# Writing attention planes and normalised-input planes to DRAM from ScalarE's queue instead of SyncE's

## The chip, the cores and the metric

The kernel runs on one core of one Trainium2 chip. The metric is the device time of one execution in microseconds; the time given for a kernel is the median of its runs.

A core has a matrix engine (TensorE, PE in the profile; its weight loads are PEld), three engines for element-wise work (VectorE or DVE, ScalarE or ACT, GpSimd or POOL), and SyncE (SP), which only issues transfers. Every engine works through its own instructions in the order in which the program gives them. Transfers between on-chip memory (SBUF) and DRAM are issued by one of the engines and then carried out by 16 DMA engines.

## The reference

Two layers, each with a pre-normalisation and a residual, on x of 128 batches x 128 nodes x 512 features in float32. The first mixes the nodes with a normalised adjacency matrix, the second is graph attention with 8 heads and an additive mask.

```python
h = relu(layernorm(x))
x = x + norm_adj @ (h @ W0) + b0
h = relu(layernorm(x))
q, k, v = (h @ Wq + bq), (h @ Wk + bk), (h @ Wv + bv)     # 8 heads of 64
attn = softmax(q k^T / 8 + (1 - adj) * -1e9)
x = x + (attn @ v) @ Wo + bo
```

## The kernel before, in words

The 128 batches go in 32 groups of four (`GB`). A group takes part in four dense products with 512 x 512 weights: first the layer-0 weight (block W), then q, k and v (blocks Q, K, V) and the output projection (block Y). Each product is a two-level fast matrix multiplication with seven block products, so a block has seven steps, Q0 to Q6 and so on; each step has a place before it (Q3) and places after its products (Q3b). All five products share the lines L388 (PE), L429 and L439 (VectorE adds block results out of the PSUM banks a, b, c, d) and, for q, k and v, L711, L714 and L725 (ScalarE takes the first result out of a bank).

Time runs in slots t. In slot t the blocks are W for group t + 1, Q, K and V for group t, and Y for group t - 1. Beside these dense blocks lie the smaller steps of neighbouring groups, put by hand into places (`at(t, place, f, ...)`). The scheduler is switched off (`manual_schedule`), so the order of each engine's instructions is the order in which these calls are made.

The names and lines on which the text below relies:

- `load_x` (L161, SP) loads half a group of x, two batches, two groups ahead into one of eight buffers. `store_half` (L838, SP) stores half a group of the result; the load of a later group takes the buffer that such a store frees.
- `ln1` (L314 and after, VectorE; L320 and L322, GpSimd) makes the statistics of the first normalisation, and `gcn_norm` (L333, ScalarE) the normalised batch `h`. `gcn_mix` (L605, PE) multiplies `h`, loaded as weights, with the adjacency matrix into `pa`; L610 (ScalarE) copies it out. In slots 2 to 29 `gcn_norm` for the four batches of group t + 2 stands at Q3, Q4, Q5b and Q6, `gcn_mix` at Q5, Q6, K1 and K2.
- `scores` (L754 PE; L758 or L761) and `row_max` (L773) begin the softmax; `exponentials` (L781, ScalarE, eight heads one by one with their sums) and `softmax_end` (L788 VectorE, L789 GpSimd) finish it.
- The normalised attention weights have to be transposed[...]. So `split_att` has ScalarE copy the float32 weights of a batch into two planes of 16-bit halves, which overwrite the attention buffer of the batch before (L794), and then sends the planes to DRAM (L795). `turn_att` (L798, SP) brings them back transposed. `attend` (L820, PE) uses them in block V of the next slot.
- In steady slots the planes of batch 0 and 1 of group t are split in block Y of that slot (Y3b) and in block W of the next (W1b), and those of batches 2 and 3 in the next slot at Q3b and Q5b. Some batches at the beginning and at the end are transposed on PE instead (`turned_in_place`).
- `split_h` and `turn_h` do the same for batches 0 and 1 of the input of attention: copies at L682 into one common pair of planes (places V2b and V3), after the second of which the planes go to DRAM (L684); L689 brings them back transposed.
- `reload_w` (L1004, SP) loads weights again in four parts each, into two buffers in turn, as PE lets their parts go.
- `Operands.combine` (L362 to L365, L90, GpSimd in steady slots) adds and subtracts operand blocks for the fast multiplication; `add_bias` (L337) and `add_mask` (L769) also run on GpSimd.

All transfers of the kernel before are issued from SP, in one order. A transfer's issue waits on SP until its source is ready and its destination is free, and whatever stands behind it on SP waits as well.

Of the kernel before, what the change touches and what calls it, by code (L numbers as in the profile page):

```python
# [93 lines left out]
def kernel(  # L94
# [16 lines left out]
    nc = tc.nc  # L111
# [36 lines left out]
    planes_dram = [dp.tile([P, 2, H * P], U16, tag=f"planes_{b}", name=f"planes_{b}") for b in range(GB)]  # L148
    h_dram = dp.tile([P, 2, H * P], U16, tag="planes_h", name="planes_h")
# [527 lines left out]
    def split_h(g, b):  # L677


        h2 = hs.pop((g, b)).bitcast(U16).rearrange("n (c f z) -> n z c f", c=NC, z=2)  # L680
        planes = att_of(g - 1, -1).bitcast(U16).rearrange("n h k -> n (h k)")
        nc.scalar.copy(planes.rearrange("n (z c j f) -> n z c j f", z=2, c=NC, j=2)[:, :, :, b, :], h2)  # L682
        if b == 1:
            nc.sync.dma_start(h_dram, planes.rearrange("n (z f) -> n z f", z=2))  # L684

    def turn_h(g):
        op_h[g] = op_norm
# [47 lines left out]
    def att_of(g, b):  # L735


        return att_buf[(b - g) % (GB + 1)]
# [52 lines left out]
    def split_att(g, b):  # L791
        halves = att_of(g, b).bitcast(U16).rearrange("q h (k z) -> q z (h k)", z=2)
        planes = att_of(g, b - 1).bitcast(U16).rearrange("q h k -> q (h k)").rearrange("q (z j) -> q z j", z=2)
        nc.scalar.copy(planes, halves)  # L794
        nc.sync.dma_start(planes_dram[b], planes)  # L795

    def turn_att(g, b):
        nc.sync.dma_start_transpose(out=att_of(g, b - 1).bitcast(U16), in_=planes_dram[b].rearrange("q z j -> (q z) j"))  # L798
# [49 lines left out]
    for t in range(-1, NG + 1):  # L848
# [3 lines left out]
        if 0 <= t - 1 < NG - 1:  # L852
            g = t - 1

            for first, final, place, f, *args in (
                ("W1", "-Y6", "Q0", turn_att, 0),
                ("W4b", "-Y6b", "W1b", split_att, 1),
                ("W5", "-Y3", "W2", exponentials, 2, 0, H // 2),
                ("W6", "-Y4", "W3", exponentials, 2, H // 2, H),
                ("Q0b", "-Y5b", "W4b", softmax_end, 2),  # L860
                ("Q1", "-Y5", "W5", exponentials, 3, 0, H // 2),
                ("Q2", "-Y6", "W6", exponentials, 3, H // 2, H),
                ("Q0", "Q1", "Q2", turn_att, 1),
                ("Q2b", "Q0b", "Q0b", softmax_end, 3),
                ("Q4b", "Q0b", "Q3b", split_att, 2),
                ("Q6b", "Q2", "Q5b", split_att, 3),
                ("K1", "Q2", "K0", turn_att, 2),
                ("K3", "Q5", "K2", turn_att, 3),
            ):
                place = first if t == 1 else final if last else place  # L870
                if f in (split_att, turn_att) and turned_in_place(g, args[0]):
                    continue
                at(t - place.startswith("-"), place.strip("-"), f, g, *args)
            if t == 1:
                at(1, "K3", transpose_att, g, 2)
                at(1, "K5", transpose_att, g, 3)
            elif last:
                at(t, "K1", transpose_att, g, 3)
            for b in (2, 3, 0, 1):
                at(t, "V0", attend, g, b)  # L880
# [15 lines left out]
        elif 1 <= t + 1 < NG and t >= 0:  # L896
            g = t + 1
            at(t, "K0b" if g < NG - 1 else "Q0b", ln2, g, 0)
            at(t, "K3b" if g < NG - 1 else "Q3b", ln2, g, 1)
            if g == NG - 1:  # L900

                places = ("Q3", "Q4", "Q5", "Q5", "Q6", "Q6", "K1", "K2", "K2")
                steps = ((norm_h, 0), (norm_h, 1), (transpose_h, 0), (norm_h, 2), (transpose_h, 1), (norm_h, 3))
                steps += ((transpose_h, 2), (transpose_h, 3))
            else:
                places = ("V1", "V2", "V2b", "V3", "V5", "V6", "Y1", "Y2", "Y5")
                steps = ((norm_h, 0), (norm_h, 1), (split_h, 0), (split_h, 1), (norm_h, 2), (norm_h, 3))
                steps += ((transpose_h, 2), (transpose_h, 3))
                at(t, "Y0", turn_h, g)
            for place, (f, b) in zip(places, steps):  # L910
                at(t, place, f, g, b)
            at(t, places[8], attention_operands, g)
            at(t + 1, "Q3", attention_residual, g, 0)
            at(t + 1, "Q4", attention_residual, g, 1)
# [263 lines left out]
```

## Time and profile before

| | |
|---|---|
| time, median of 3 runs | 2293.26 us (2292.56 to 2294.22) |
| span of the profiled execution | 2291.6 us |
| time of the profiled execution around the span | not recorded |
| granted TensorE clock | 0.998 |
| busy: PE, PEld | 99%, 93% |
| busy: VectorE, ScalarE, GpSimd | 82%, 60%, 81% |
| SP's DMA queue (q1) | 448336 packets, 560.08 MB, 80.6% of 16 engines |
| plane writes issued on SP | L795: 121 of 512 KB, 4.5 us to landing; L684: 29 of 512 KB, 3.0 us |

The profile is of one execution. Its times run from the start of its first instruction. "Busy" is the share of the span in which an engine worked on an instruction; issuing a transfer doesn't count as busy. A timeline line gives the start, the length, the engine, the source line, the operation, what it writes and reads, and in brackets how long its engine stood idle before it and what ended that. A line of the list of waits gives who waited for whom: microseconds in total, times, the longest.

### The profile page before, as it was taken

The numbers are of one execution on the slowest core, as the hardware profiler recorded it, in microseconds if no ns is written. First come the engines' busy times: TensorE is split into PE (matmuls) and PEld (weight loads), VectorE is DVE, ScalarE is ACT, GpSimd is POOL, SyncE is SP. The second block draws the span as 40 slices with busy tenths as digits, with TensorE's granted clock in tenths as the row PEclk, the third lists the DMA queues.
The fourth block names the chain that finished last, engine by engine and source line by source line (L and its number), as shares of the span: only waits on it lengthen the run. The fifth ranks groups of instructions, "written<-read, shape, count | busy, mean of one in ns | idle before, by whom it ended". The sixth has DMA issues, their size and how long they took to land.

```text
span 2291.6 us, 50617 instructions
## 1 busy us (share of the span) xinstructions
PE 2273.9 (99%) x18151; PEld 2132.9 (93%) x18151; DVE 1868.3 (82%) x4832; ACT 1364.3 (60%) x3556; POOL 1860.9 (81%) x1927
## 2 busy tenths in 40 slices
PE   9899999999999999999999999999999999999999
PEld 8899999999999999999999999999999999999998
DVE  7877888888888788887888888888888888888876
ACT  3555565655656556656556565565665665655654
POOL 6899788878888788888888887879888888878854
PEclk9999999999999999999999999999999999999999
DMA  5388978889887889878898788998888987889872
GB/s 169 157 259 245 298 231 256 239 251 280 250 252 241 254 254 276 257 247 236 251 297 243 250 238 250 270 258 260 244 246 252 291 253 236 243 245 291 239 242 81
DMA packets 448587, 563.32 MB, mean 246 GB/s; under 512 B 326352, under 2 KB 333648, under 8 KB 447824
## 3 DMA queue, kind: packets, MB, share of 16 engines
q1 hardware_dynamic: 448336, 560.08, 80.6%
q8 instruction: 144, 2.36, 0.4%
q14 instruction: 107, 0.88, 0.1%
HBM read 358.68 MB, written 122.68 MB: 210 GB/s over the span
## 4 chain that ended last, share of the span: by engine, by line
PE 88%; POOL 3%; DMA 3%; DVE 3%; issue 1%; ACT 1%; SPq 0%; POOLq 0%; DVEq 0%; ACTq 0%
PE bank_a L388 31%; PE bank_d L388 19%; PE bank_c L388 10%; PE bank_b L388 10%; PE pa L605 5%; PE bank_d L754 3%; PE po L820 3%; DMA xt<-in_x_dram 2%; PE pss L754 1%; PE bank_b L820 1%; PE bank_a L820 1%; PE bank_b L754 1%; PE pt L674 1%; POOL xt L337 1%; DVE xt L429 1%
## 5 line engine op out<-in xcount | busy, mean ns | idle before, releaser
L781 ACT ACTIVATE att<-att,nmx 128x128 f32<-128x128 f32 x1024 | 396.3, 391 | 0.9 <-DVE nmx L773 0.9
L388 PE MATMUL bank_a<-op_h,w 128*128 128x256 f32 x1488 | 352.0, 379 | 0.0
L789 POOL TENSOR_TENSOR att<-att,rsm 128x1024 f32<-128x1024 f32 x128 | 242.7, 1897 | 82.3 <-DVE rsm L788 82.3
L388 PEld LDWEIGHTS bank_a<-op_h,w 128*128 128x128 f32 x1488 | 268.9, 190 | 29.0
L429 DVE TENSOR_TENSOR xt<-xt,bank_d 128x512 f32<-128x512 f32 x732 | 269.0, 416 | 19.0 <-DVE xt L429 0.9
L794 ACT COPY att<-att 128x2048 uint16<-128x2048 uint16 x121 | 229.3, 1895 | 66.0 <-POOL att L789 66.0
L333 ACT ACTIVATE h<-xt,nb,rs 128x512 f32<-128x512 f32 x254 | 207.2, 817 | 57.8 <-POOL nb L322 56.1
L711 ACT ACTIVATE q<-bank_a,bqk 128x256 f32<-128x256 f32 x192 | 80.4, 470 | 263.0 <-PE bank_a L388 263.0
L320 POOL TENSOR_TENSOR rs<-ve,mhalf 128x2 f32<-128x2 f32 (+1 forms) x129 | 91.4, 708 | 176.2 <-DVE ve L319 175.8
L388 PE MATMUL bank_d<-op_h,w 128*128 128x128 f32 (+1 forms) x1712 | 218.2, 279 | 0.7 <-issue 0.3
L90 POOL TENSOR_TENSOR op_o<-op_o 128x256 f32<-128x256 f32 x297 | 209.6, 729 | 10.0
L388 PEld LDWEIGHTS bank_d<-op_h,w 128*128 128x128 f32 x1712 | 204.0, 193 | 5.1 <-issue 3.1
L90 POOL TENSOR_TENSOR op_a<-op_a 128x256 f32<-128x256 f32 x279 | 196.8, 729 | 14.1 <-DVE op_a L365 4.5
L90 POOL TENSOR_TENSOR op_h<-op_h 128x256 f32<-128x256 f32 x270 | 190.4, 729 | 12.2 <-DVE op_h L365 2.9
L781 ACT ACTIVATION_READ_ACCUMULATOR att<-att,nmx 128x1 f32 x1024 | 194.1, 190 | 0.0
L314 DVE BATCH_NORM_STATS2 st<-xt 128x6 f32<-128x512 f32 x256 | 173.0, 676 | 18.4 <-DMA xt<-in_x_dram 18.3
L388 PE MATMUL bank_a<-w,op_o 128*128 128x256 f32 x768 | 181.7, 379 | 0.0
L388 PE MATMUL bank_a<-w,op_h 128*128 128x256 f32 x744 | 179.1, 384 | 0.0
L388 PE MATMUL bank_a<-w,op_a 128*128 128x256 f32 x744 | 176.1, 380 | 0.0
L439 DVE TENSOR_TENSOR xt<-bank_a,xt 128x512 f32<-128x512 f32 x252 | 167.2, 684 | 10.2 <-PE bank_a L388 2.7
L761 DVE SCALAR_TENSOR_TENSOR att<-bank_d,msk 128x512 f32<-128x512 f32 x128 | 82.5, 686 | 104.4 <-PE bank_d L754 96.8
L773 DVE TENSOR_REDUCE nmx<-att 128x8 f32<-128x1024 f32 x128 | 155.0, 1211 | 0.0
(188 smaller groups left out, 5944.3 us busy)
## 6 DMA issues: line engine op xcount, KB each, us to landing
w<-wd_v SPq DMA_DIRECT2D x93, 704.0 KB, 5.5
w<-wd_o SPq DMA_DIRECT2D x93, 704.0 KB, 6.8
w<-wd_q SPq DMA_DIRECT2D x90, 704.0 KB, 6.1
planes<-att SPq DMA_DIRECT2D x121, 512.0 KB, 4.5
w<-wd SPq DMA_DIRECT2D x87, 704.0 KB, 5.4
xt<-in_x_dram SPq DMA_DIRECT2D x63, 512.0 KB, 6.1
out_dram<-xt SPq DMA_DIRECT2D x62, 512.0 KB, 4.2
planes_h<-att SPq DMA_DIRECT2D x29, 512.0 KB, 3.0
```

The source lines that it names most:

```text
L90: engine.tensor_tensor(twice(out), twice(x), twice(y), ALU.subtract if minus else ALU.add)
L314: nc.vector.bn_stats(self.st[:, j, :], self.src[:, j, :])
L333: nc.scalar.activation(h, src[:, j, :], AF.Relu, bias=nb[:, j : j + 1], scale=rs[:, j : j + 1])
L388: nc.tensor.matmul(out, lhsT, rhs, start=start, stop=True, skip_group_check=True)
L429: nc.vector.tensor_tensor(dst, dst, src, f)
L439: nc.vector.tensor_tensor(t, src.rearrange("p (r f) -> p r f", r=2), t, ALU.add)
L605: nc.tensor.matmul(pa[:, c * P : (c + 1) * P], h[:, c * P : (c + 1) * P], ant, start=True, stop=True)
L754: nc.tensor.matmul(pss[p][:, c, :], qs[g][rows, c, cols], ks[g][rows, c, cols], start=True, stop=True)
L773: nc.vector.tensor_reduce(nmx, att_of(g, b), AX.X, ALU.max, negate=True)
L781: nc.scalar.activation(att[:, h, :], att[:, h, :], AF.Exp, bias=nmx[:, h : h + 1], scale=1.0, accum_out=sm[:, h : h + 1])
L789: nc.gpsimd.tensor_tensor(att, att, rsm.unsqueeze(2).to_broadcast([P, H, P]), ALU.mult)
L794: nc.scalar.copy(planes, halves)
```

## The change

Two plane writes change their issuing engine: that of the normalised input (`split_h`) and that of the attention weights (`split_att`). Each call is at the same place in the program, right after the ScalarE copy that makes the planes. The transposing reads (`turn_h`, `turn_att`) stay on SP, as do all other transfers.

```diff
@@ -681,7 +681,7 @@
         planes = att_of(g - 1, -1).bitcast(U16).rearrange("n h k -> n (h k)")
         nc.scalar.copy(planes.rearrange("n (z c j f) -> n z c j f", z=2, c=NC, j=2)[:, :, :, b, :], h2)
         if b == 1:
-            nc.sync.dma_start(h_dram, planes.rearrange("n (z f) -> n z f", z=2))
+            nc.scalar.dma_start(h_dram, planes.rearrange("n (z f) -> n z f", z=2))
@@ -792,7 +792,7 @@
         halves = att_of(g, b).bitcast(U16).rearrange("q h (k z) -> q z (h k)", z=2)
         planes = att_of(g, b - 1).bitcast(U16).rearrange("q h k -> q (h k)").rearrange("q (z j) -> q z j", z=2)
         nc.scalar.copy(planes, halves)
-        nc.sync.dma_start(planes_dram[b], planes)
+        nc.scalar.dma_start(planes_dram[b], planes)
```

In the program as built, ScalarE's order has 150 more instructions, each right behind the copy of L794 or the second copy of L682, and SP's order has 150 fewer. The orders of PE, VectorE and GpSimd are the same as before.

## The prediction

> **What bounds the kernel now.** First the page's busy times, then the lists of waits of TensorE and VectorE.
>
> ```profile
> PE 2273.9 (99%) x18151; PEld 2132.9 (93%) x18151; DVE 1868.3 (82%) x4832; ACT 1364.3 (60%) x3556; POOL 1860.9 (81%) x1927
> ...
> PEld bank_c L388 <- DVE xt L429: 10.9, 16, 4.2
> ...
> PE bank_c L388 <- DVE xt L429: 7.4, 8, 3.8
> ...
> DVE st L314 <- DMA xt<-in_x_dram: 18.3, 19, 2.4
> ```
>
> TensorE (PE) is idle for 2291.6 - 2273.9 = 17.7 us in all, the prologue included. So whatever the change does well can bring back less than 1%, while whatever makes PE wait is lost in full. Its one wait that recurs is for VectorE to empty bank c (L429), and that follows VectorE's wait for x's load: L314 stands in VectorE's order ahead of the read that PE needs.
>
> Next the chain of waits in order of time, by which I measure the period: the same instruction, `po` L820, once per group of four batches.
>
> ```profile
> 846.87 1.90 PE po L820 x32
> ...
> 916.95 1.90 PE po L820 x32
> ...
> 987.02 1.90 PE po L820 x32
> ...
> 1058.28 1.78 PE po L820 x29
> ```
>
> The distances are 70.08, 70.07 and 71.26 us. From 213.09 to 2112.35 us there are 27 such distances: 1899.26 us, against 27 x 70.07 = 1891.89 at the shortest. All that steady stages lose now is 7.4 us, in the groups in which x's load lands late. This is the most that a better DMA order can return there.
>
> Last the place where a delay of ScalarE (ACT) has no cover: the timelines of ACT, of PE's weight loads and of PE around the split of batch 3.
>
> ```profile
> 900.90 0.84 ACT L711 ACTIVATE q<-bank_a,bqk 128x256 f32<-128x256 f32 x2 [0.95 <-PE bank_a L388]
> 901.62 1.90 ACT L794 COPY att<-att 128x2048 uint16<-128x2048 uint16 x1
> 903.41 0.82 ACT L333 ACTIVATE h<-xt,nb,rs 128x512 f32<-128x512 f32 x1
> ...
> 904.29 1.01 PEld L605 LDWEIGHTS pa<-ant,h 128*128 128x128 f32 x8
> ...
> 902.71 1.89 PE L388 MATMUL bank_a<-op_h,w 128*128 128x256 f32 x8
> 904.43 1.05 PE L605 MATMUL pa<-ant,h 128*128 128x128 f32 x8
> ```
>
> Columns are start, length, engine, line. The third `h` of the group ends at 903.41 + 0.82 = 904.23, and the load of it as PE's weights begins at 904.29, 0.06 later: that load waits for `h`. The first product follows 0.14 later, exactly when the product before it lets PE go. At two other places a load stands 0.11 ahead of its first product (907.23 and 907.34), so `h` has 0.14 - 0.11 = 0.03 us to spare. Other groups show the same picture (974.31 and 974.36; 1045.56 and 1045.61; 1115.66 and 1115.71).
>
> **What the Trainium skill says.** "DMA: Bandwidth & Descriptors", section "Issuing engines are not separate DMA queues": whichever engine issues, transfers share the same 16 DMA engines, and another issuer saves only issue time. The trace of before has SP's queue alone, so it can't confirm this. "Perfetto Trace Analysis", section "DMA Instruction — HWDGE (DVE, Sync)": the recorded issue covers a wait for the descriptor generator, locked "for exclusive use", and the generating; moving the data comes after. The trace agrees on the second half: issues of 0.34 us land after 3.0 us. "PSUM — Partial Sum Buffer", section "Engine vs sequencer instructions": ScalarE's queue is strict FIFO. The timeline agrees, in program order throughout. "ScalarE: Activation LUTs", section "What ACT_TABLE_LOAD costs": back-to-back ACTIVATEs overlap by about 93 ns; the trace has 903.52 - 903.41 = 0.11 us.
>
> **The change, part by part.** 150 DMA issues (121 of L795, 29 of L684) leave SP and stand in ACT's order right behind the copy whose result they send. They wait for that copy. Their other waits (an earlier use of the same DRAM plane, and in the third site x's second load, landed by about 898) are over by then. Transfers and bytes stay.
>
> *Price of one issue on ACT.* Before has none there, so I price it from SP's rows.
>
> ```profile
> L795 SPq DMA_DIRECT2D planes<-att x121: 332/428/1507, 113.7 to 2216.1; - x121
> ...
> L798 SPq DMA_TRANSPOSE att<-planes x121: 1555/4079/8754, 118.2 to 2224.3; - x121
> ```
>
> (Minimum/median/maximum in ns.) Lost overlap 0.11; the copy's end to the issue's start 0.05 (903.52 to 903.58 on SP); the issue 0.43, the median; restart 0.05, the gap between two issues on SP (874.31 to 874.36). Sum 0.64 us. From below: with an issue and restart of nothing it is 0.16, never less, because the wait for the copy is certain. From above: 0.11 + 0.05 + 1.51 + 0.15 = 1.8 us, or more if the issue waits for a transpose (rival 2).
>
> *Where it lies.* Normalised input (L684, 860.6 us in the group from 846.87): behind it is the copy of v that PE needs at 862.37; it ends at 861.10, so 1.27 us are spare: covered. The exponentials after it end at 864.2 + 0.6, before VectorE's reciprocal at 864.98: covered. Planes of batches 0 and 1 (copies end at 873.94 and 877.91): ACT idles 7.2 us ahead of the q bias at 891.28 and swallows 2 x 0.64: covered. Batch 2 (copy ends at 898.76): behind it the second `h`, needed at 900.48 and done at 899.47; then ACT idles 0.95 ahead of the L711 at 900.90. 0.64 is covered, above 0.95 it is not. Batch 3 (copy ends at 903.52): no cover, as shown. PE waits 0.64 - 0.03 = 0.61 us, and all that follows moves with it; the fourth `h` is needed at 907.34 and was done at 905.42.
>
> This last site exists where batch 3 is split and the next group is mixed, slots t = 2 to 29: 28 times. 28 x 0.61 = +17 us.
>
> *What SP gains.* From its list of waits:
>
> ```profile
> SPq L684 <- ACT att L682: 471.0, 29, 18.3
> ...
> SPq L795 <- ACT att L794: 144.4, 61, 3.5
> SPq L161 <- DMA out_dram<-xt: 138.8, 28, 6.4
> ```
>
> The first two go from SP. Behind L684 stood the first weight reload (issued at 861.11, its old readers done at 857.7), behind L795 another: they move up by about 3 us into a stretch in which DMA had room (share 0.69 from 872 to 880). The planes of batch 1 go out at 878.5 instead of 880.24. But x's load (L161, issued at 883.34) follows the store of x, which waits for VectorE's last L429, and that does not move. What is late next is that store and the bytes issued from 878 on, the same as before. What disappears is a backlog: planes of batch 0 and a reload, 1.2 MB from 873.97 on, last at the page's 246 GB/s until 879.0, some 0.6 us into that store; moved up, they are through by then. So I expect the load to land about 0.6 us earlier. VectorE's typical wait is 18.3/19 = 1 us, so about half of the 7.4 us goes: -4 us; bounds 0 and -7.4. The transposes of batches 2 and 3 (L798) start no later; their result is needed at 916.88, covered.
>
> *Sum.* +17 - 4 = +13 us on the profiled execution. Its span is 2291.6 us; its own whole time is not recorded, so I take the 1.7 us up to the median of 2293.3 as what lies around the span. 2293.3 + 13 = 2306.
>
> **Rivals.** (1) *Faster, or no change.* SP's queue was the brake and ACT has room: 60% busy, long idle stretches. Then all 7.4 us come back, and the first steady group's 2 us (72.1 against 70.07) too, so -9.4. The deciding point is ACT's delay at batch 3: at its floor of 0.16 it costs 28 x 0.13 = 3.6, net -6, 2287 us. With all the gain, break-even is at 9.4/28 + 0.03 = 0.37 us of delay; the net reaches the 0.2% bound (4.6 us) on the fast side only below 0.2 us. For it: the waits of 471 and 144 us on SP. Against it: most of the 471 hid nothing late on PE, and no plane's issue took under 0.33 us on SP.
>
> (2) *Slower by far: ACT's issue waits for the descriptor generator while SP issues a transpose.* At batch 2 SP is inside one:
>
> ```profile
> 896.97 4.58 SPq L798 DMA_TRANSPOSE att<-planes  x1
> 901.65 0.53 SPq L795 DMA_DIRECT2D planes<-att  x1
> ```
>
> Held from 898.81 to 901.55, ACT would be 2.74 us later: 0.64 + 2.74 - 0.95 = 2.4 beyond the cover, x 28 = +68; 2306 + 68 = 2374 us. If only part of the instruction holds it, some 0.5 us at each of the two sites: (0.19 + 0.5) x 28 = +19, 2325. Against it: the direct issue right behind that transpose took 0.53 us, only 0.19 more than the shortest, so little is queued up at its end.
>
> (3) *Nothing measurable.* An issue on ACT takes about half of SP's (delay 0.35): 28 x 0.32 = 9, less 7.4: +1.6, 2295 us. That the change does nothing is excluded: the order of both queues differs.
>
> **How the numbers follow.** The forecast (slower by 5 to 20 us) has 0.60, rival 2 in either size 0.12, the no-change case 0.16, the faster one 0.12. About 0.2%, 4.6 us, is what a measurement of this kernel can tell from no change. Faster 0.12, same 0.16, slower 0.72. Range: below, into the no-change case with all of the DMA gain, 2291; above, issue rows of 0.53 with a slow restart and no gain (28 x 0.8 = +22) and the smaller size of rival 2, 2326. What is left out is the faster case and the full lock.
>
> **What would show it.** In the changed profile: ACT's own queue with 150 issues near 0.4 us; the third `h` about 0.6 us after the copy's end instead of before it; a new wait of PE or PEld at `pa` L605 on ACT `h` L333, some 28 times and about 17 us in total; a shortest period of 70.7 us; VectorE's wait for x's load halved; ACT's busy time unchanged. I am wrong if `pa` shows no wait (then the issue is cheap or the order has slack that I missed), if ACT's issues are long (rival 2), or if a shorter period appears, which would mean that the present 70.07 us hides a wait for SP.

## The result and the profile after

The changed kernel takes 2299.69 us (median of 7 runs, 2297.68 to 2301.03) against 2292.56 us of the kernel before beside it (7 runs, 2291.01 to 2294.22): ratio 1.0034, 95% interval 1.0023 to 1.0044. It is 7.1 us slower. The profiled execution of it took 2300.85 us with a span of 2299.1 us, so 1.75 us lie around the span, as had been assumed.

The busy times and the two queues, from the page of the changed kernel:

```profile
PE 2276.8 (99%) x18151; PEld 2130.3 (93%) x18151; DVE 1867.7 (81%) x4832; ACT 1372.3 (60%) x3556; POOL 1860.7 (81%) x1927
...
q1 hardware_dynamic: 426736, 481.43, 70.5%
q10 hardware_dynamic: 21600, 78.65, 8.9%
```

A second queue, q10, carries the 78.65 MB of planes. The shares of busy time are the same to a point and don't tell what happened.

The chain of waits of the changed kernel, again the same instruction once per group:

```profile
848.92 1.90 PE po L820 x32
...
919.57 1.90 PE po L820 x32
...
990.11 1.90 PE po L820 x32
...
1060.66 1.90 PE po L820 x32
```

From 213.96 to 2118.93 us there are 27 distances, 1904.97 us, 70.55 on average; 26 of the 27 lie within 0.05 us of that. Before, the shortest was 70.07 and the mean 70.34. So two things happened at once. Every group became 0.48 us longer than the shortest one before, 13.1 us over the 27; and the uneven extra of some groups, 7.4 us before, is gone. The net is 5.7 us; the remaining 1.8 us of the difference of the spans lie in equal parts ahead of the first and behind the last of these groups.

The waits of PE's weight loads and of VectorE say what the two things are. From the changed kernel's lists of waits:

```profile
PEld pa L605 <- ACT h L333: 19.2, 30, 1.2
PEld bank_c L388 <- DVE xt L429: 6.0, 6, 4.2
```

```profile
DVE st L314 <- DMA xt<-in_x_dram: 4.0, 4, 2.5
```

The first line is new: 30 waits for `h`, none of which is in the list of before. VectorE's wait for x's load fell from 19 times to 4, and PE's loads wait for bank c 6 times instead of 16.

Where the new wait arises: the timelines of ScalarE and of PE's weight loads in the group from 848.92.

```profile
903.77 1.90 ACT L794 COPY att<-att 128x2048 uint16<-128x2048 uint16 x1
905.70 0.34 ACTq L795 DMA_DIRECT2D planes<-att  x1
906.08 0.81 ACT L333 ACTIVATE h<-xt,nb,rs 128x512 f32<-128x512 f32 x1 [0.42 <-ACT att L794]
```

```profile
906.95 0.97 PEld L605 LDWEIGHTS pa<-ant,h 128*128 128x128 f32 x8 [0.61 <-ACT h L333]
```

The copy ends at 905.67. The issue starts 0.03 later, takes 0.34, and `h` starts 0.04 after it. Before, `h` started 0.11 ahead of the copy's end. Together `h` is 0.03 + 0.34 + 0.04 + 0.11 = 0.52 us later, of which 0.03 was spare: 0.49 us for PE, against the 0.48 by which the distance grew.

### The profile page after: what moved, and what is told of

Read it like the earlier page. It is cut to its first block, busy times and chain, and to the rows that moved or that the text cites. A ratio compares the mean times of both kernels' runs of the same rounds, so it can differ in the third digit from the quotient of the medians.

```text
span 2299.1 us, 50449 instructions
## 1 busy us (share of the span) xinstructions
PE 2276.8 (99%) x18151; PEld 2130.3 (93%) x18151; DVE 1867.7 (81%) x4832; ACT 1372.3 (60%) x3556; POOL 1860.7 (81%) x1927
## 3 DMA queue, kind: packets, MB, share of 16 engines
q10 hardware_dynamic: 21600, 78.65, 8.9%
## 4 chain that ended last, share of the span: by engine, by line
PE 91%; ACT 5%; DVE 2%; issue 1%; ACTq 0%; DMA 0%; SPq 0%; POOL 0%; DVEq 0%; POOLq 0%
PE bank_a L388 33%; PE bank_d L388 22%; PE bank_b L388 10%; PE bank_c L388 10%; PE pa L605 4%; PE bank_d L754 3%; PE po L820 3%; ACT att L794 2%; PE pt L674 1%; PE pss L754 1%; PE bank_b L820 1%; PE bank_a L820 1%; PE bank_b L754 1%; ACT h L333 1%; ACT q L711 1%
## 5 line engine op out<-in xcount | busy, mean ns | idle before, releaser
L794 ACT COPY att<-att 128x2048 uint16<-128x2048 uint16 x121 | 229.3, 1895 | 65.2 <-POOL att L789 65.2
```

## The experiments

All times are medians; the kernel before ran beside each batch on the same chip (2291.51, 2292.06 and 2291.3 us in the three batches). "Over the shortest" is what 27 distances exceed 27 x 70.07 us by, in the profiled execution: 7.4 us before, 13.1 us after the change.

**Batch 3 back on SP.**

```diff
-        nc.scalar.dma_start(planes_dram[b], planes)
+        (nc.sync if b == 3 else nc.scalar).dma_start(planes_dram[b], planes)
```

> The changed kernel, but the planes of batch 3 are written from SP again; all others stay on ScalarE. Theory (the loss is the one issue ahead of the third h, the gain is x's load landing earlier): PE's wait at pa for h goes, the shortest and the usual period are 70.07 us, x's load keeps its earlier landing, so about 7 us less than before: 2285.5 us (2284 to 2288). Rival A (the loss is spread over all 121 + 29 issues on ScalarE, or comes from two queues sharing the DMA engines): one fifth of the 121 goes, so still above before, 2297 to 2299. Rival B (SP's order is what brings x's load forward, and putting one write back on it undoes that): 2292, period again varying between 70.07 and 71.3.

Measured: 2286.64 us, ratio to the kernel before 0.9978 (0.9969 to 0.9986), 0.3 us over the shortest. The list of waits of its weight loads has 2 waits for `h` instead of 30:

```profile
PEld pa L605 <- ACT h L333: 1.0, 2, 0.9
```

One of the five issues of a group carries the whole loss, and the other four the whole gain. Rival A and rival B both fall.

**Batch 3 alone on ScalarE.** The same condition turned around, in the kernel before.

> The kernel before, but the planes of batch 3 alone are written from ScalarE. Theory: the wait at pa comes in full, 28 x 0.48 = 13 us, and nothing is gained on x's load, so 2292.6 + 13 = 2306 us (2303 to 2308): slower than the changed kernel, though it moves only 29 of 150 writes. Rival A (loss spread over all issues): a fifth of the loss, 2294 to 2296. Rival B (two queues at once are the gain, whatever is on them): about 2299, like the changed kernel.

Measured: 2306.1 us, ratio 1.0063 (1.005 to 1.0075), 14.6 us slower. Its shortest distance is 70.55 and it is 17.7 us over the shortest: the loss, with the late loads of x still there. It moves a fifth of the writes and is slower than moving all.

```profile
PEld pa L605 <- ACT h L333: 18.8, 29, 1.7
PEld bank_c L388 <- DVE xt L429: 9.2, 13, 4.1
```

**All on ScalarE, `h` ahead of the split.** In the changed kernel the steady place of the split of batch 3:

```diff
-                ("Q6b", "Q2", "Q5b", split_att, 3),
+                ("Q6b", "Q2", "Q6", split_att, 3),
```

> The changed kernel with all 150 writes on ScalarE, but in steady slots the split of batch 3 stands one place later, so that ScalarE makes the third h first and then the copy and its write. Theory: the third h is ready at about 902.4 instead of 904.8 in the reckoning of the group from 846.87, PE's wait at pa goes, period 70.07, 2285.5 us (2284 to 2288), the same as with batch 3 on SP. Rival A (the number of issues on ScalarE or the second queue costs time): 2299, as changed. Rival C (the next thing on ScalarE is just as tight: the fourth h or the copy of pa): a new wait of PE at the fourth pa or at bank d, 2289 to 2296.

Measured: 2286.26 us, ratio 0.9977 (0.9968 to 0.9987), 0.5 us over the shortest. Its timeline of ScalarE:

```profile
896.89 0.81 ACT L333 ACTIVATE h<-xt,nb,rs 128x512 f32<-128x512 f32 x1
897.60 1.89 ACT L794 COPY att<-att 128x2048 uint16<-128x2048 uint16 x1
899.51 0.34 ACTq L795 DMA_DIRECT2D planes<-att  x1
899.90 0.58 ACT L610 COPY op_a<-pa 128x512 f32<-128x512 f32 x1 [0.41 <-PE bank_a L388]
900.38 0.81 ACT L333 ACTIVATE h<-xt,nb,rs 128x512 f32<-128x512 f32 x1
```

The third `h` now comes ahead of the copy, the fourth behind the issue, and in the steady groups nothing new waits. So neither the number of issues on ScalarE nor the second queue costs time: only which instruction stands behind the issue.

**Two issues instead of one at batch 3.** In the changed kernel:

```diff
+        if b == 3:
+            for z in range(2):
+                nc.scalar.dma_start(planes_dram[b][:, z, :], planes[:, z, :])
+        else:
+            nc.scalar.dma_start(planes_dram[b], planes)
```

> The changed kernel, but the planes of batch 3 go out in two writes of half the size, both from ScalarE, one behind the other. Theory (PE pays each issue in full): one more issue of 0.34 us and a gap of 0.05, so PE's wait grows by 0.39 x 28 = 11 us to 2310.6 us (2308 to 2313), period about 70.94. Rival D (what PE pays is the draining of the copy, the issue itself overlaps with what follows): unchanged, 2299 to 2301.

Measured: 2317.08 us, ratio to the kernel before 1.0108 (1.0092 to 1.0123), 17.4 us above the changed kernel where 11 were expected. The wait grows, so PE pays the issue itself and rival D falls. The usual distance is 71.04 us, 0.49 more than after the change: the two issues and their gap take 0.82 us where one takes 0.34, and that is 0.09 more than reckoned, because the second one takes at least 0.44.

```profile
911.49 0.82 ACTq L797 DMA_DIRECT2D planes<-att  x2
912.36 0.81 ACT L333 ACTIVATE h<-xt,nb,rs 128x512 f32<-128x512 f32 x1 [0.90 <-ACT att L794]
```

The rest is in a few groups in which the pair took up to 1.92 us, the longest single issue 1.53 us. In some of these SP was inside a transpose and in others not; why they are long is open.

**Only the normalised input on ScalarE.** L684 alone, in the kernel before.

> The kernel before, with the normalised-input planes alone (29 writes) written from ScalarE. Theory: ScalarE has cover at that site and SP's long wait for it hid nothing that is late, so no change: 2291.5 us (2290 to 2293), x's load still late in about half of the groups. Rival E (SP's 471 us of waiting for those planes was the brake): the whole gain, 2286.

Measured: 2291.77 us against 2292.06, ratio 0.9999 (0.999 to 1.0007); VectorE waits for x's load 18 times. SP's longest wait of all, 471 us in total, was worth nothing, and the issue on ScalarE there costs nothing: the cover named for this site held.

**Only batches 0 and 1 on ScalarE.**

```diff
-        nc.sync.dma_start(planes_dram[b], planes)
+        (nc.scalar if b < 2 else nc.sync).dma_start(planes_dram[b], planes)
```

> The kernel before, with the planes of batches 0 and 1 alone (60 writes) written from ScalarE. Theory: these are the writes that stand ahead of x's load on SP, and ScalarE idles 7 us behind them; the whole gain at no cost: 2286.5 us (2285 to 2288), period 70.07. Rival E (the brake was elsewhere on SP): 2290 to 2292.

Measured: 2285.04 us, ratio 0.9969 (0.9958 to 0.9981), 0.6 us over the shortest: the whole gain, and the lowest ratio of the study, though its interval overlaps those of the first and the third run.

**Four issues at batch 2.** Batch 3 on SP, and for batch 2 four writes of a quarter each in place of one:

```diff
+            for k in range(4):
+                z, cols = k // 2, slice(k % 2 * 512, k % 2 * 512 + 512)
+                nc.scalar.dma_start(planes_dram[b][:, z, cols], planes[:, z, cols])
```

> Batch 3 on SP as in the first experiment, all others on ScalarE, and the planes of batch 2 in four writes of a quarter each, one behind the other on ScalarE. Theory (0.95 us of ScalarE's time behind batch 2 are covered, then PE pays in full): one issue delays by 0.53 us and each further one by 0.48, the value of the two-issue run, so 0.53 + 3 x 0.48 = 1.97, of which 1.0 is beyond the cover: 28 x 1.0 = 28 us on top of 2286.6, 2314 us (2308 to 2320), with PE waiting at the second pa of the group. Rival F (every issue on ScalarE in this stretch costs PE): three issues more than in the first experiment, 40 us, 2327. Rival G (cover is larger than that, the wait is only at batch 3): 2286.6.

Measured: 2324.97 us, ratio 1.015 (1.0136 to 1.0164), 38.3 us above the first experiment where the theory had 28 and rival F 40. The median alone would favour the rival; the profile doesn't. The median of its distances is 71.08 us, 1.01 above 70.07, just what the cover of 0.95 leaves (rival F would be 71.5), and PE waits at the second `pa` of the group, as expected:

```profile
983.09 1.16 PE L605 MATMUL pa<-ant,h 128*128 128x128 f32 x8 [0.69 <-ACT h L333]
```

Over 27 distances it has 29.8 us over the shortest, against 0.3 in the first experiment. The other 9 us are outside the steady groups: the first of them begins at 215.94 instead of 211.7 us, behind one wait of PE's loads for `h` of 3.3 us, and 5 us come behind the last, whose cause is open. The reckoning had left both out.

**Only batch 1 on ScalarE.** The condition `b == 1`.

> The kernel before, with the planes of batch 1 alone (31 writes) written from ScalarE, so that the weight reload still waits on SP behind the planes of batch 0. Theory of the prediction (the gain comes from planes of batch 0 and the reload behind it moving up into a stretch in which the DMA engines have room): less than half of the gain, 2289 to 2291.5. Rival H (the gain comes from the write of batch 1 itself, which no longer goes out right ahead of the store and x's load in the same queue): the whole gain, 2286.5.

Measured: 2287.06 us, ratio 0.9978 (0.997 to 0.9986), 1.2 us over the shortest; VectorE waits for x's load 8 times instead of 19:

```profile
DVE st L314 <- DMA xt<-in_x_dram: 5.5, 8, 1.9
```

One write of the five brings 5.0 of the 7.0 us that the sixth run gains over the same runs of the kernel before. That is rival H in the main: the step of the prediction that put the gain on batch 0 and the reload behind it fails. What can be theirs is the rest, 2.0 us.

**Batch 1 earlier, but on SP.** The kernel before, with the place of the split of batch 1 moved so that only SP's order changes:

```diff
-                ("W4b", "-Y6b", "W1b", split_att, 1),
+                ("W4b", "-Y6b", "W0", split_att, 1),
```

> The kernel before, all writes on SP, but in steady slots the write of batch 1 is issued ahead of two weight reloads instead of behind them, so at about 878.8 instead of 880.24 in the reckoning of the group from 846.87; nothing else moves. Theory H1 (on ScalarE the write of batch 1 gains because it goes out earlier): most of the gain of batch 1 alone, about 2287 to 2288.5 us. Theory H2 (it gains because it is out of the queue in which the store and x's load follow): no gain, 2291 to 2293, since the same bytes stand ahead of x's load in SP's queue.

**Batch 1 behind the exponentials, on ScalarE.** The kernel before, with the call that writes batch 1 moved to ScalarE and placed behind the exponentials of batch 2 (cut to the lines that matter):

```diff
-        nc.sync.dma_start(planes_dram[b], planes)
+        if not (b == 1 and 1 < g + 1 < NG - 1):
+            nc.sync.dma_start(planes_dram[b], planes)
...
+        nc.scalar.dma_start(planes_dram[1], planes)
...
+                at(t, "W3", send_planes, g)
```

> The kernel before, with the write of batch 1 alone issued from ScalarE in slots 2 to 30, but behind the eight exponentials that follow its copy, so at about 881 instead of 878.4, later than SP issued it before (880.24). Theory H1 (earlier is what counts): no gain, 2291 to 2294 us. Theory H2 (another queue is what counts): most of the gain, 2286 to 2288.5, with x's load landing about 7.2 us after its issue instead of 8.0.

Measured: the earlier write on SP 2290.23 us, ratio 0.9994 (0.9986 to 1.0002), not to be told from no change, 3.8 us over the shortest in its profile. The write behind the exponentials on ScalarE 2288.08 us, ratio 0.9986 (0.9978 to 0.9995), 2.2 us over the shortest.

The tenth run is not the test that it was meant to be: its write did not go out later than before. Its call stands behind the eight exponentials in the program, but in the trace the issue starts during the third of them, in the group whose first `po` product starts at 843.55:

```profile
872.76 1.90 ACT L794 COPY att<-att 128x2048 uint16<-128x2048 uint16 x1 [2.06 <-POOL att L789]
...
875.35 0.39 ACT L781 ACTIVATE att<-att,nmx 128x128 f32<-128x128 f32 x1
875.52 0.37 ACTq L800 DMA_DIRECT2D planes<-att  x1
875.64 0.19 ACT L781 ACTIVATION_READ_ACCUMULATOR att<-att,nmx 128x1 f32 x1
```

That is 31.97 us after the first `po` product. SP issued this write at 33.4 in the kernel before, here in the group from 846.87:

```profile
880.24 0.44 SPq L795 DMA_DIRECT2D planes<-att  x1
```

So H1 is not refuted by this run. The table has the moment of the write beside the landing of x's first load of a group, means over the 27 steady groups of each trace:

| kernel | batch 1's write issued, us after the first `po` product | x's load, issue to landing, us | over the shortest, us |
|---|---|---|---|
| before | 33.44 on SP | 8.02 | 7.4 |
| batch 1 earlier, on SP | 32.06 on SP | 7.83 | 3.8 |
| batch 1 behind the exponentials | 31.97 on ScalarE | 7.61 | 2.2 |
| batch 1 alone on ScalarE | 31.15 on ScalarE | 7.18 | 1.2 |
| batches 0 and 1 on ScalarE | 31.14 on ScalarE | 7.04 | 0.6 |
| changed kernel | 31.14 on ScalarE | 7.02 | covered by the new wait |

Being earlier on the same queue brings at most a part (ninth run). At nearly the same moment the kernel is 2.15 us faster with the write on ScalarE than on SP (2288.08 against 2290.23 us, side by side on one chip). Whether that is the other queue itself is open: with one issue fewer ahead of them, two weight reloads leave SP 0.5 and 0.9 us earlier than in the ninth run. From ScalarE 0.8 us earlier still, the eighth run gains more. How the queue and the moment share the gain is not shown.

The tenth run shows one more thing. There the issue costs ScalarE nothing: the eighth exponential ends 34.20 us after `po`, as in the kernel before, and at 34.81 in the eighth run, where the issue stands directly behind the copy and has to wait for it.

The load is issued at the same point of the group in all of them (36.5 us after `po`; in the tenth run one group, left out, has it 2.3 us later). The store of x ahead of it lands sooner too: 5.90 us after its issue in the changed kernel, 7.13 before. Not everything does: the group's first store takes 4.36 us instead of 3.47, and x's second load 4.74 instead of 4.14.

## Why the prediction was right, and where its sizes and one reason were not

**Right: the direction, the place and the mechanism.** PE waits at the third `pa` of the group for `h`, behind the issue at batch 3, about 0.5 us in each group. The second experiment shows that issue to cause it, the first and third that nothing else does.

**The price of one issue** was put at 0.64 us from SP's median row of 0.428. It is 0.52: the issue takes ScalarE 0.338 us, in the 121 issues of L795 never over 0.375. SP's median mixed two kinds of rows. The 43 plane writes that stood directly behind another issue of SP took 0.41 us or more, and the other 107 have a median of 0.34; on ScalarE all 150 follow a pause. Of the 0.12 us too much 0.09 is the issue, and 0.03 the two gaps around it (0.03 and 0.04 us instead of 0.05 each). So 28 x 0.49 = 13.7 us instead of 17.

**What SP gains** was put at half of 7.4 us; it is all of it, and x's load lands 1.0 us earlier where 0.6 was reckoned. And its reason failed. The prediction saw the write of batch 1 go out earlier, but took the bytes issued from 878 on to be "the same as before", so that the only gain was a backlog of batch 0 and a reload that moves up. The eighth run leaves both where they were and has 5.0 of the 7.0 us. What helps is that the write of batch 1 leaves its place right ahead of the store and x's load: it goes out on another queue, and 2.3 us earlier, since on SP it stood behind a store and two reloads. There was room for it: from 31 to 36 us after `po` the DMA engines' busy share is 0.87 in the kernel before and 0.96 in the eighth run (means over the 27 steady groups). What counted was when and on which queue the bytes went, not their sum. How the DMA engines share their time between two queues no run shows directly.

Both errors go the same way: +13.7 - 7.4 = +6.3 on the steady groups against +13 predicted, and with what lies around the steady groups +7.1 measured. The direction did not hang on the half of the gain that was left out: with all of the gain the prediction's own break-even was 0.37 us of delay, and the delay is 0.52.

**The covers held.** The normalised input costs nothing (fifth run). Batches 0 and 1 cost nothing (sixth run). Batch 2 is covered up to 0.95 us (seventh run, whose steady groups lose what is above that). The transposes of batches 2 and 3 start no later, as said: 57.5 and 61.5 us after `po` (medians), 58.5 and 62.7 before. ScalarE's busy time was said not to change; it rose by 8.0 us.

**The rivals.** The faster one had the gain right in full, but it needed a delay of under 0.2 us, and the delay is 0.52. The lock of the descriptor generator, by far the worst case, doesn't occur: of the 150 issues on ScalarE 32 begin inside a transpose that SP is issuing, and they take 0.34 to 0.37 us like the others. In the group from 848.92 SP is in one from 898.46 to 903.53, and batch 2's issue inside it is of the shortest kind:

```profile
900.93 0.34 ACTq L795 DMA_DIRECT2D planes<-att  x1
```

```profile
898.46 5.07 SPq L798 DMA_TRANSPOSE att<-planes  x1
```

So for one issue at a time the "exclusive use" of the Trainium skill ("Perfetto Trace Analysis", section "DMA Instruction — HWDGE (DVE, Sync)") does not show as a wait as long as the other queue's instruction. Its statement that another issuer saves only issue time ("DMA: Bandwidth & Descriptors", "Issuing engines are not separate DMA queues") no run here decides: every write that helped from ScalarE's queue also went out earlier, or let SP's next issues go out earlier.

## What to carry to other kernels

Price an issue that moves to a computing engine by the instruction right behind it: find the instruction that reads that one's result, and subtract what it has to spare. Here 0.34 us of issuing was free at four places in the group and cost PE 0.49 us at the fifth, and on the old queue a write with 471 us of waiting was worth nothing to move, while one that it hardly waited for was worth 5.0 of the 7.0 us. So move writes one by one. Where one has no cover, change the order of two instructions before giving up the move (third run), or put the call behind work that the engine already has in hand, so that the wait for its source is over by then (tenth run; not tried at batch 3).

## What the runs showed of the hardware that had not been expected

- An issue of a 512 KB write on ScalarE takes 0.338 us, also while SP issues a transpose, and delays the next instruction behind the copy by 0.52 us in all. A second issue directly behind it (256 KB each) takes 0.44 us typically, never less, and up to 1.53.
- Placed behind eight exponentials, when its copy was done, such an issue started during the third of them and delayed none (the last ends 34.20 us after `po` with it and without).
- Moving one write of 512 KB per group to another queue, which also sent it 2.3 us earlier, let a store and a load that had followed it land about 1 us earlier (7.13 to 6.16 and 8.02 to 7.18 us), with the same bytes to move.
